# Two graph-attention layers: dense products of both layers in pieces of 512 columns that run across the relations

## The chip, the cores and the metric

The kernel runs on one core of a Trainium2 chip. The metric is the device time of one execution in microseconds, as a median over runs. A core has five engines with queues of their own: PE (TensorE, the matrix products; its weight loads are listed apart as PEld), DVE (VectorE), ACT (ScalarE), POOL (GpSimd) and SP (SyncE, which only issues transfers here). Each engine works through its queue in order and waits for others by semaphores.

## The reference

x has 3125 nodes of 768 features. There are 53125 edges (source, destination, relation 0 to 2, sorted by destination). Two layers of relational graph attention follow one another, then x is added and a layer norm taken. One layer, cut to what matters:

```python
xr = jnp.einsum('nd,rdf->rnf', x, W)          # three relations, 768 x 768 each
oi, oj = xr[etype, dst], xr[etype, src]
alpha = leaky_relu(oi @ q + oj @ k, 0.2)      # per edge and head
e = jnp.exp(alpha - segment_max(alpha, dst)[dst])
a = e / (segment_sum(e, dst)[dst] + 1e-16)
out = segment_sum(a[:, :, None] * oj.reshape(-1, heads, out_ch), dst) + b
```

Layer 1 has four heads of 192 columns, layer 2 one head of 768. Between them stands an elu. The dense product `xr` is the largest piece of arithmetic: 3125 x 768 times 768 x 2304 in each layer.

## The kernel before

**Blocks and stages.** The nodes are cut into 25 blocks of 128 (NB). Four stages follow one another: preparation (`weights_kq`, `nodes_kq`), `phase1` (dense product of layer 1, attention weights of layer 1), `phase2` (sums of layer 1 over the edges, elu, dense product of layer 2) and `phase3` (attention weights and sums of layer 2, layer norm). The order of all instructions is written out by hand: each stage is a loop over small steps, a table `ev` holds what is emitted at which step, and every engine executes its share in that order.

**A dense product.** A float32 product is made of three products in fp32r: a high part of x times a high and a low part of W (`wH`, `wL`), and a low part of x times the high part of W. The 768 rows of W make six tiles (DT), so one output piece takes 6 x 3 = 18 matmuls into one PSUM buffer `po`, of which there are two. `wH` and `wL` hold W as [128, 18 tiles, 770]. A piece has half the columns of one relation (384), so a block takes 3 relations x 2 halves x 18 = 108 matmuls. In layer 2 the first half of each relation is 386 wide: columns 384 and 385 hold W2·k and W2·q.

**Layer 1** (`phase1`, loop over n). One step emits one piece: `d_group` (L724) emits 18 matmuls, and `d_row` in the next step emits ACT's copy of the piece to a row buffer (L743) and, after the second half, SP's store of the row to `tab1` (L745). Rows have 772 columns: per head 192 and a one. Three row buffers rotate. Each sixth matmul is made to wait for one of the indirect gathers of attention keys that POOL issues meanwhile (L479), the same fraction along their list. Block b's x is transposed by `d_turn` (L701) and split into high and low by `d_split` (ACT L708, DVE L709). Between the pieces PE, DVE and ACT make the attention weights (`a_index` to `a_put`); `a_back` (L683) transposes what ACT's exp (L679) made behind two DVE scans. The last four blocks run relation by relation, so that each relation's part of `wH` and `wL` comes free and can take W2. `w_split` splits W2 and stores it to `w2_d` earlier; `second_weights` loads it in twelve transfers on ACT's queue (L532), four for each relation, and DVE puts `wkq2` into columns 384 and 385 (L534, L535). Block 0's layer-1 product is made in `nodes_kq` (L403) in pieces of 384.

**Layer 2** (`phase2`, loop over k, one gathered slot of 128 edges per step, 17 steps per block). POOL gathers rows of `tab1`; DVE makes selection matrices (`high`, L471); PE multiplies them with the gathered rows into `acc` (`sums`, L978), in two batches per block. When a block's second batch is done, a chain of small steps makes its h: DVE `e_y` (L986 to L991), ACT `e_x` (L997), DVE `e_h` (L1022, L1023) giving `ey`, PE `e_t` (six transposes, L1030), ACT `e_s` (L1037) and DVE `e_s2` (L1043), which give the high and the low half of `hT`. Then its dense product starts (`d_part`, L1055): 18 parts per block, six matmuls each, spread over 17 steps. `d_part` of the block before is emitted between the links of this chain, since a block's parts run from six steps behind its own chain's start to five steps behind the next one's. `d_row` copies a piece to one of three row buffers (L1063), DVE picks the query column (L1067), SP stores the row to `tab2` (L1069).

**Layer 2's sums** (`phase3`) gather rows of `tab2` and multiply them in the same way (L1260, L1272), 386 columns twice.

Of the kernel before, what the change touches and what calls it, by code (L numbers as in the profile page):

```python
# [60 lines left out]
def kernel(  # L61
# [85 lines left out]
    wkq2 = keep.tile([P, R * DT, 2], F32, name="wkq2")  # L147
# [149 lines left out]
    def weights_kq(buf, work, psum, bank, kqr, wk, kqs, wH, wL, nodes, more):  # L297
# [8 lines left out]
        def turn(m):  # L306
            raw = [buf["W", 2 * m + c] for c in range(2)]
            pts = transposes(psum, raw)
            for c in range(2):
                i = 2 * m + c  # L310
                S.copy(wH[:, i, :D], raw[c])
                (V if i % 3 == 2 else G).tensor_sub(wL[:, i, :D], raw[c], wH[:, i, :D].bitcast(F32))
                buf.free("W", i)
            return split_parts(work, pts, 2 * P)
# [33 lines left out]
    def nodes_kq(buf, pre, work, psum, bank, wk, kqs, wH, wL, qq, more, edges_ready):  # L348
# [43 lines left out]
        def first(i):  # L392
# [8 lines left out]
            for t in (2 * i, 2 * i + 1):  # L401
                for n, (a, w) in enumerate(((tH, wH), (tH, wL), (tL, wH))):
                    T.matmul(po[g][:, :HALF], a[:, t % 2, :], w[:, r * DT + t, c * HALF:(c + 1) * HALF],  # L403
                             start=(t == 0 and n == 0), stop=(t == DT - 1 and n == 2))
# [121 lines left out]
    def second_weights(r, wH, wL):  # L526

        i = slice(r * DT, (r + 1) * DT)
        w = w2_d[r * DT * P:(r + 1) * DT * P, :].rearrange("(i p) (s c f) -> p s i c f", p=P, s=2, c=2)
        for c in range(2):  # L530
            for s, o in ((0, wH), (1, wL)):
                nc.scalar.dma_start(o.bitcast(F32)[:, i, c * HW:c * HW + HALF], w[:, s, :, c])  # L532
                yield
        V.tensor_copy(wH[:, i, HALF:HW], wkq2[:, i])  # L534
        V.tensor_sub(wL[:, i, HALF:HW], wkq2[:, i], wH[:, i, HALF:HW].bitcast(F32))  # L535


    def phase1(pre, work, psum, wH, wL, qq):
# [175 lines left out]
        def d_group(n, b, r, c):  # L714

            g, k = divmod(n, 6)
            po = psum.tile([P, 512], F32, name="po", bufs=2)
            xT = xt[b]
            n = 0
            for t in range(DT):  # L720
                i = r * DT + t
                sl = slice(c * HALF, (c + 1) * HALF)
                for s, w in ((0, wH), (0, wL), (1, wH)):
                    m = T.matmul(po[:, :HALF], xT[:, s, t, :], w[:, i, sl], start=(n == 0), stop=(n == 3 * DT - 1))  # L724
                    if n % 6 == 0:
                        tc.add_manual_dep(m.ins, gathered[slot((18 * g + 3 * k + n // 6) * NE // (3 * len(groups)))].name,
                                          behind, reason="an even load")
                    n += 1
            st["po", b, r, c] = po

        n_rows = []
        row_of = {}

        def d_row(b, r, c):
            po = st.pop(("po", b, r, c))
            if c == 0:
                n_rows.append(b)
                row_of[b, r] = rows[len(n_rows) % 3] if (b, r) != (NB - 1, R - 1) else share[3]
                if (b, r) == (NB - 1, R - 1):
                    V.memset(share[3].rearrange("p (h f) -> p h f", h=H1)[:, :, F1:CW], 1.0)  # L740
            o = row_of[b, r]
            to = o.rearrange("p (h f) -> p h f", h=H1)[:, 2 * c:2 * c + 2, :F1]
            S.copy(to, po[:, :HALF].rearrange("p (h f) -> p h f", h=2))  # L743
            if c == 1:
                nc.sync.dma_start(  # L745
                    tab1[b * P * R:(b + 1) * P * R, :].rearrange("(p r) f -> p r f", r=R)[:, r, :], o)
                if b == 1:

                    nc.sync.dma_start(tab2[N * R:, :].rearrange("(p r) f -> p r f", r=R)[:, r, :], o)
# [12 lines left out]
        def w_split(i):  # L762
            w = w2.pop(i)
            hl = work.tile([P, 2, D], F32R, name="w2hl", bufs=1)
            S.copy(hl[:, 0, :], w)
            V.tensor_sub(hl[:, 1, :], w, hl[:, 0, :].bitcast(F32))
            for s in range(2):
                j = work.tile([P, D], BF, name="w2j", bufs=1)
                V.scalar_tensor_tensor(j, w, 1.0, kq2[:, s, :], op0=ALU.mult, op1=ALU.mult,
                                       accum_out=wkq2[:, i, s:s + 1])  # L770
# [35 lines left out]
        groups = [(b, r, c) for b in range(1, GB) for r in range(R) for c in range(2)]  # L806
        groups += [(b, r, c) for r in range(R - 1) for b in range(GB, NB) for c in range(2)]
        groups += [(b, R - 1, c) for c in range(2) for b in range(GB, NB)]
# [3 lines left out]
        turn = [base(b) * len(groups) // NE for b in range(NB - LATE)]  # L812
# [32 lines left out]
        last_w2 = second_weights(R - 1, wH, wL)  # L845
        for n in range(max(ev) + 1):
# [15 lines left out]
            if m in (9, 17):  # L862
                w2s = second_weights(m // 16, wH, wL)
            if 9 <= m < 25:
                next(w2s, None)
            if m in (21, 22):
                next(last_w2)
# [5 lines left out]
            if n < len(groups):  # L873
                d_group(n, *groups[n])
            if 0 < n <= len(groups):
                d_row(*groups[n - 1])
            if n == len(groups):
                next(last_w2)
                next(last_w2)
        return last_w2  # L880


    def phase2(work, psum, wH, wL, last_w2):
# [1124 lines left out]
```

## Time and profile before

| | |
|---|---|
| median of 3 runs | 1987.32 us (1985.41 to 1988.5) |
| profiled execution | 1984.63 us, span 1982.8 us |
| PE busy | 1680.7 us, 85% |
| DVE busy | 1201.9 us, 61% |
| ACT busy | 376.5 us, 19% |
| POOL busy | 1333.2 us, 67% |
| DMA | 506.48 MB, mean 255 GB/s |
| chain that ended last | PE 60%, issue 10%, POOL 8%, DMA 7%, DVE 5% |
| of it dense products | layer 2 (L1055) 25%, layer 1 (L724) 20% |

The page's fifth part lists groups of instructions: line, engine, operation, tiles and shapes, count, then busy time, mean duration of one, and the engine's idle time before them. A matmul's duration there (344 ns for 386 columns) contains its way through the array; in a stream the next one ends sooner, so the distance between neighbours tells what one costs.

Times in the timeline count from the start of the span. Layer 1's products run from about 123 to 655 us, layer 2's from 691 to 1397, and layer 2's sums from 1401 to the end.

### The profile page before, as it was taken

The page shows a single profiled execution, that of the slowest core. Times are in us where ns is not written, and L with a number is a line of the kernel's source. Part 1 is how long each engine was busy: PE and PEld are TensorE (multiplying, and loading weights), DVE is VectorE, ACT ScalarE, POOL GpSimd, SP SyncE. Part 2 cuts the span into 40 slices and gives each one's busy share as a digit, 9 for nine tenths or more (in the row PEclk, how much of TensorE's full clock was granted, in tenths as well). Part 3 has the DMA queues.
Part 4 walks back from the last instruction along what each step waited for, and adds up shares of the span by engine and source line. Part 5 has one row for each costly group of instructions (what it writes and reads, how often), then busy time and mean ns, then how long its engine had stood idle before and what let it go on. Part 6 is the DMA issues. An engine that isn't in the chain of part 4 may idle for free.

```text
span 1982.8 us, 41452 instructions
## 1 busy us (share of the span) xinstructions
PE 1680.7 (85%) x14727; PEld 1406.6 (71%) x14727; DVE 1201.9 (61%) x4296; ACT 376.5 (19%) x661; POOL 1333.2 (67%) x1326
## 2 busy tenths in 40 slices
PE   6989999999999599999999999999465556556664
PEld 6979999999999489898989999899222223223322
DVE  6544555555554667767776777774456665666564
ACT  5421222221221011111111111111011211121111
POOL 4247777777771467777777776652577777777773
PEclk8989999999999899999999999999677777777777
DMA  7556545554557988888888888886799999999994
GB/s 196 191 122 189 179 162 187 170 167 159 182 186 242 365 274 272 294 271 278 272 297 268 276 273 297 271 277 215 252 322 334 331 334 347 335 318 317 327 321 145
DMA packets 161018, 506.48 MB, mean 255 GB/s; under 512 B 47925, under 2 KB 61244, under 8 KB 160803
## 3 DMA queue, kind: packets, MB, share of 16 engines
q0 software_dynamic: 81904, 331.52, 50.6%
q1 hardware_dynamic: 67101, 156.21, 22.3%
q10 hardware_dynamic: 11798, 16.00, 2.5%
q8 instruction: 120, 1.97, 0.4%
q14 instruction: 95, 0.78, 0.1%
HBM read 412.74 MB, written 95.69 MB: 256 GB/s over the span
## 4 chain that ended last, share of the span: by engine, by line
PE 60%; issue 10%; POOL 8%; DMA 7%; DVE 5%; ACT 1%; POOLq 0%; DVEq 0%; ACTq 0%; SPq 0%
PE po L1055 25%; PE po L724 20%; PE acc L978 10%; POOL G L479 8%; DMA G<-ftab,ridx 6%; PE acc L1260 2%; PE pt L1030 1%; DVE selp L471 1%; PE px L701 1%; PE acc L1272 1%; DVE share L674 0%; DVE F L1219 0%; DMA share<-ftab,rfirst 0%; DVE share L675 0%; DVE sT L624 0%
## 5 line engine op out<-in xcount | busy, mean ns | idle before, releaser
L1055 PE MATMUL po<-wH,hT 128*128 128x386 f32 (+1 forms) x1800 | 485.0, 344 | 3.1 <-DVE hT L1043 2.2
L479 POOL DMA_INDIRECT kt<-kt,ridx x374 | 397.4, 1062 | 113.9 <-issue 106.6
L479 POOL DMA_INDIRECT G<-ftab,ridx x374 | 376.2, 1006 | 113.9 <-issue 99.3
L724 PE MATMUL po<-wH,xT 128*128 128x384 f32 x1584 | 435.7, 346 | 5.5 <-ACT share L743 2.4
L471 DVE TENSOR_SCALAR selp<-frow,fdl,pall 128x32 f32<-128x32 f32 (+1 forms) x1688 | 384.0, 321 | 0.7 <-PE acc L978 0.7
L1055 PEld LDWEIGHTS po<-wH,hT 128*128 128x128 f32 x1800 | 330.5, 189 | 18.8 <-issue 14.7
L479 POOL DMA_INDIRECT share<-ftab,ridx x239 | 239.2, 1001 | 100.7 <-PE acc L978 47.4
L1055 PE MATMUL po<-wL,hT 128*128 128x386 f32 (+1 forms) x900 | 305.6, 340 | 0.0
L724 PEld LDWEIGHTS po<-wH,xT 128*128 128x128 f32 x1584 | 292.9, 190 | 9.3 <-ACT share L743 4.2
L724 PE MATMUL po<-wL,xT 128*128 128x384 f32 x792 | 269.5, 340 | 0.0
L1260 PE MATMUL acc<-G,selp 128*32 128x386 f32 x2292 | 249.2, 584 | 6.6 <-DVE selp L471 6.6
L1260 PEld LDWEIGHTS acc<-G,selp 128*32 128x32 f32 x2292 | 126.8, 128 | 102.7 <-issue 53.7
L479 POOL DMA_INDIRECT g<-ftab,ridx x135 | 135.2, 1001 | 64.5 <-PE acc L978 34.0
L978 PE MATMUL acc<-share,selp 128*32 128x193 f32 x3088 | 165.7, 330 | 13.5 <-DVE selp L471 11.1
L1063 ACT COPY r<-po 128x386 f32<-128x386 f32 (+1 forms) x150 | 72.3, 482 | 550.5 <-PE po L1055 550.5
L1055 PEld LDWEIGHTS po<-wL,hT 128*128 128x128 f32 x900 | 170.6, 190 | 0.0
L724 PEld LDWEIGHTS po<-wL,xT 128*128 128x128 f32 x792 | 151.1, 191 | 0.0
L978 PEld LDWEIGHTS acc<-share,selp 128*32 128x32 f32 x3088 | 114.0, 111 | 48.0 <-issue 22.0
L1171 DVE TENSOR_SCALAR sT<-bc,cols 128x512 bf16<-128x512 f32 (+1 forms) x125 | 82.5, 660 | 89.4 <-PE bc L1165 89.4
L743 ACT COPY share<-po 128x384 f32<-128x384 f32 x144 | 68.0, 479 | 298.9 <-PE po L724 278.2
L1165 PE MATMUL bc<-d,one 1*128 1x512 bf16 (+1 forms) x125 | 50.1, 400 | 87.2 <-DVE sT L1171 86.1
L978 PE MATMUL acc<-g,selp 128*32 128x193 f32 x1688 | 102.8, 328 | 1.5 <-DMA g<-ftab,rfirst 1.5
(288 smaller groups left out, 1923.5 us busy)
## 6 DMA issues: line engine op xcount, KB each, us to landing
ftab<-share SPq DMA_DIRECT2D x75, 386.0 KB
ftab<-r SPq DMA_DIRECT2D x75, 386.0 KB
share<-in_L_gnn_W_dram SPq DMA_DIRECT2D x36, 384.0 KB
w_d<-w2hl SPq DMA_DIRECT2D x18, 768.0 KB
sT<-dr_d SPq DMA_DIRECT2D x25, 534.0 KB
share<-in_x_dram SPq DMA_DIRECT2D x27, 384.0 KB
xb_d<-share SPq DMA_DIRECT2D x25, 384.0 KB
xr<-in_x_dram SPq DMA_DIRECT2D x21, 384.0 KB
```

The costliest lines, as they stand in the source:

```text
L471: V.tensor_scalar(sel.rearrange("p (t f) -> p t f", f=32), of, dl[:, b, j:j + 1], p, op0=ALU.is_equal, op1=ALU.mult)
L479: return G.indirect_dma_start(out=to, out_offset=None, in_=tab, in_offset=_index(i[:, j:j + 1]), bounds_check=NP * R - 1, oob_is_err=False)
L701: T.transpose(pt[:, t // 3, (t % 3) * P:(t % 3 + 1) * P], xr[:, t * P:(t + 1) * P], ident)
L724: m = T.matmul(po[:, :HALF], xT[:, s, t, :], w[:, i, sl], start=(n == 0), stop=(n == 3 * DT - 1))
L743: S.copy(to, po[:, :HALF].rearrange("p (h f) -> p h f", h=2))
L978: T.matmul(acc[32 * t:32 * t + 32, h // 2, c], sel[:, h, 32 * WINDOW[i].index(t):][:, :32], g[:, h * CW:(h + 1) * CW], start=(i == u[0] an ...
L1030: T.transpose(pt[:, t // 3, (t % 3) * P:(t % 3 + 1) * P], s["ey"][:, t * P:(t + 1) * P], ident)
L1055: T.matmul(po[:, :wd], hT[:, k, t, :], w[:, r * DT + t, sl], start=(t == 0 and n == 0), stop=(t == DT - 1 and n == 2))
L1063: S.copy(o[:, c * HW:c * HW + wd], po[:, :wd])
L1165: T.matmul(bc[:, :n], one, s["d"][:, 4 * i * P:4 * i * P + n], start=True, stop=True)
L1171: V.tensor_scalar(s["sT"][:, 4 * i * P:4 * i * P + n], bc[:, :n], cols[:, b:b + 1], None, op0=ALU.is_equal)
L1260: T.matmul(acc[32 * t:32 * t + 32, c, :HW], st[b, j][:, 32 * WINDOW[j].index(t):][:, :32], gs[:, (base(b) + j) % NG, c * HW:(c + 1) * HW], ...
```

## The change

`wH` and `wL` become [128, 6 tiles, 2310]: in each tile six columns for W·k and W·q (KQ = 6, k in reversed order of relations), then the 768 columns of each relation one after another. The dense products go over these columns in pieces of 512 whatever the relation: 512, 512, 512, 512, 256 in layer 1 and 512, 512, 512, 512, 262 in layer 2 (there with the six columns in front). A block takes 5 x 18 = 90 matmuls. In layer 1 a step emits 15 of them, in layer 2 a part emits five. `d_row` cuts a piece at relations and, in layer 1, at heads; a piece's copy in layer 1 is emitted six matmuls behind its last one. The layer-1 dependences on gathers stand at each fifth matmul. Rows of `tab2` now begin with the key column, then 768 columns, then the one. W2 is loaded in six column parts of two transfers each, behind the pieces of the last four blocks, and `wkq2` is copied once. In those blocks five row buffers rotate, and `d_turn` and `d_split` of the last three come in successive steps.

```diff
-    def second_weights(r, wH, wL):
+    def second_weights(r, f, n, wH, wL):
+        w = w2_d[r * DT * P:(r + 1) * DT * P, :].rearrange("(t p) (s f) -> p s t f", p=P, s=2)
+        for s, o in ((0, wH), (1, wL)):
+            nc.scalar.dma_start(o.bitcast(F32)[:, :, KQ + r * D + f:][:, :, :n], w[:, s, :, f:f + n])
+            yield
...
-        def d_group(n, b, r, c):
...
+        PIECES = [(f, min(512, R * D - f)) for f in range(0, R * D, 512)]
+        def d_products(groups):
+            made = 0
+            for b, (f, n) in groups:
+                po = psum.tile([P, 512], F32, name="po", bufs=2)
+                xT = xt[b]
+                i = 0
+                for t in range(DT):
+                    for s, w in ((0, wH), (0, wL), (1, wH)):
+                        m = T.matmul(po[:, :n], xT[:, s, t, :], w[:, t, KQ + f:KQ + f + n], start=(i == 0),
+                                     stop=(i == 3 * DT - 1))
+                        if made % 5 == 0:
+                            k = made // 5 * NE // (3 * STEPS)
+                            tc.add_manual_dep(m.ins, gathered[slot(k)].name, behind, reason="an even load")
+                        i += 1
+                        made += 1
+                        yield
+                due.append((made + 6, b, f, n, po))
...
+        later = share[:3] + [share[6], share[3]]
+        def d_row(b, f, n, po):
+            got = 0
+            for r, at, m in segments(f, f + n, D):
+                if at == 0:
+                    if b < GB:
+                        row_of[b, r] = rows[r]
+                    else:
+                        row_of[b, r] = later[len(n_rows) % 5]
+                        n_rows.append(b)
+                o = row_of[b, r]
+                for h, at_, k in segments(at, at + m, F1):
+                    if at_ == 0 and k == F1 and h % 2 == 0 and at + m >= (h + 2) * F1:
+                        S.copy(o.rearrange("p (h f) -> p h f", h=H1)[:, h:h + 2, :F1],
+                               po[:, got:got + 2 * F1].rearrange("p (h f) -> p h f", h=2))
+                    elif not (at_ == 0 and k == F1 and h % 2 and at <= (h - 1) * F1):
+                        S.copy(o[:, h * CW + at_:h * CW + at_ + k], po[:, got:got + k])
+                    got += k
...
+        STEPS = 6 * (NB - 1)
+        groups = [(b, p) for b in range(1, GB) for p in PIECES]
+        groups += [(b, p) for p in PIECES for b in range(GB, NB)]
...
+        w2s = {m: second_weights(r, f, n, wH, wL) for m, r, f, n in (
+            (7, 0, 0, 512), (11, 0, 512, 256), (13, 1, 0, 256), (16, 1, 256, 512), (21, 2, 0, 512), (25, 2, 512, 256))}
...
-            if m in (1, 3, 5):
-                d_turn(GB + 1 + m // 2)
-                d_split(GB + 1 + m // 2)
+            if m in (1, 2, 3):
+                d_turn(GB + m)
+                d_split(GB + m)
...
+            for u in (m, m - 1):
+                if u in w2s and m < 25:
+                    next(w2s[u])
...
+            for _ in range(15 if n <= STEPS else 0):
+                if next(products, 0) is None:
+                    made += 1
+                while due and (due[0][0] <= made or n == STEPS):
+                    d_row(*due.pop(0)[1:])
+            if n == STEPS:
+                next(w2s[25])
+                next(w2s[25])
...
+        PIECES = [(f, min(512, WW - f)) for f in range(0, WW, 512)]
+        def d_products(b):
+            s = blk[b]
+            hT = s["hT"]
+            for p, (f, n) in enumerate(PIECES):
+                po = s["po", p] = psum.tile([P, 512], F32, name="po", bufs=2)
+                i = 0
+                for t in range(DT):
+                    for k, w in ((0, wH), (0, wL), (1, wH)):
+                        T.matmul(po[:, :n], hT[:, k, t, :], w[:, t, f:f + n], start=(i == 0), stop=(i == 3 * DT - 1))
+                        i += 1
+                        yield
+        def d_part(b):
...
+            for _ in range(5):
+                next(s["parts"], None)
+        def d_row(b, p):
...
+            if p == 0:
+                s["q"] = work.tile([P, R], F32, name="q2", bufs=2)
+                s["k"] = work.tile([P, R], F32, name="k2", bufs=2)
+                V.tensor_copy(s["q"], po[:, :R])
+                V.tensor_copy(s["k"], po[:, R:KQ])
+            for r, at, m in segments(max(f, KQ) - KQ, f + n - KQ, D):
+                o = rows[r]
+                if at == 0 and r > 0:
+                    V.tensor_copy(o[:, 0:1], s["k"][:, R - 1 - r:R - r])
+                a = 1 if at == 0 and r == 0 else 0
+                got = KQ + r * D + at - f
+                S.copy(o[:, 1 + at - a:1 + at + m], po[:, got - a:got + m])
+                if at + m == D:
+                    nc.sync.dma_start(nodes(b, tab2.rearrange("(n r) f -> n r f", r=R))[:, r, :], o)
...
             for m in range(6 * R):
-                rc = divmod(m // 3, 2)
                 k = e + m * SL // (6 * R) if i else first + 5 + m * (SL + 3) // (6 * R)
-                when(k, d_part, b, *rc, m % 3)
-                if m % 3 == 2:
-                    when(k + 1, d_row, b, *rc)
+                when(k, d_part, b)
+                for p in range(len(PIECES)):
+                    if (18 * p + 17) // 5 == m:
+                        when(k + 1, d_row, b, p)
...
-                    T.matmul(acc[32 * t:32 * t + 32, c, :HW], st[b, j][:, 32 * WINDOW[j].index(t):][:, :32],
-                             gs[:, (base(b) + j) % NG, c * HW:(c + 1) * HW], start=(j == u[0]), stop=(j == u[-1]))
+                    T.matmul(acc[32 * t:32 * t + 32, c, :HALF + c], st[b, j][:, 32 * WINDOW[j].index(t):][:, :32],
+                             gs[:, (base(b) + j) % NG, 1 + c * HALF:][:, :HALF + c], start=(j == u[0]), stop=(j == u[-1]))
```

More of the change, by code (lines that the diff above doesn't have):

```diff
@@ L731, in phase1 @@
         n_rows = []
         row_of = {}
[L734 to L749, printed above, removed]
+        due = []
```

125 lines of the change are left out of this document (44 added, 81 removed).

## The prediction

> **What bounds the kernel now.** I read the table of stretches first. Its columns are the stretch, its length, then busy time and (in brackets) instructions of PE, PEld, DVE, ACT and POOL, the granted clock, DMA share and GB/s.
>
> ```profile
> 150.00:600.00 450.00, 441.89 (x2850) 430.32 (x2848) 240.06 (x711) 92.26 (x181) 350.78 (x326) 1.00 0.53 175
> 695.00:1000.00 305.00, 305.00 (x3322) 274.18 (x3322) 217.29 (x920) 47.16 (x84) 223.22 (x224) 1.00 0.84 278
> 1450.00:1980.00 530.00, 322.44 (x2882) 158.05 (x2880) 311.56 (x997) 92.11 (x118) 388.08 (x386) 0.73 0.89 314
> ```
>
> PE fills the layer-1 products (first row) and the layer-2 products (second) at full clock. The third stage, layer 2's sums, has DMA at 0.89 and PE idle for 40% of it. So the change acts where PE is the bound. Next, the chain of waits over one block of layer 2 (start, length, what, count):
>
> ```profile
> 825.15 4.09 PE acc L978 x96
> 829.24 5.47 PE po L1055 x30
> 834.71 0.75 PE pt L1030 x6
> 835.46 4.25 PE po L1055 x24
> 839.71 4.08 PE acc L978 x96
> 843.78 9.69 PE po L1055 x54
> 853.47 4.09 PE acc L978 x94
> ```
>
> One period is 28.32 us, from one second batch's end (829.24) to the next (857.56): 108 products, two batches of sums, six transposes. Then the timeline behind 829.24, with what the next block's products need:
>
> ```profile
> 829.79 1.39 DVE L991 SCALAR_TENSOR_TENSOR y<-acc,rz,fbias 128x192 f32<-128x192 f32 x4
> 831.10 1.97 DVE L471 TENSOR_SCALAR selp<-frow,fdl,pall 128x64 f32<-128x64 f32 x8
> 832.84 0.63 DVE L1022 TENSOR_SCALAR ey<-ey 128x768 f32<-128x768 f32 x1
> 833.51 0.96 DVE L1023 SCALAR_TENSOR_TENSOR ey<-y,ey 128x768 f32<-128x768 f32 x1
> 834.58 0.64 PEld L1030 LDWEIGHTS pt<-fident,ey 128*128 128x128 f32 x6 [0.19 <-issue]
> 835.49 0.80 ACT L1037 CAST hT<-pt 128x768 fp32r<-128x768 f32 x1 [1.27 <-PE pt L1030]
> 836.32 0.96 DVE L1043 TENSOR_TENSOR hT<-pt,hT 128x768 fp32r<-128x768 f32 x1
> 837.60 0.38 PEld L1055 LDWEIGHTS po<-wH,hT 128*128 128x128 f32 x2
> ```
>
> This is the latency that the products hide. DVE works without a pause from the sums' end until `ey` is ready at 834.47; the transposes start 0.11 us later, after a gap of 0.19: PE already waits a little. ACT makes the high half of `hT` by 836.29, DVE the low half by 837.28. The first product that needs the low half is a block's third; its weights load at 837.60, 0.32 later. There is almost no slack here. Last, the time of one product by width, in the PE timeline (two products per row) and the chain, and the layer-1 waits:
>
> ```profile
> 68.32 0.40 PE L293 MATMUL bank<-tH,wk 128*128 128x256 f32 x2
> 69.51 0.41 PE L293 MATMUL bank<-tL,wk 128*128 128x256 f32 x2
> 1375.91 21.13 PE po L1055 x120
> PE pa L683 <- ACT e L679: 7.6, 12, 2.1
> 662.43 1.00 POOL L479 DMA_INDIRECT share<-ftab,rfirst  x1 [55.78 <-DMA wL<-w_d]
> ```
>
> 256 columns: ten products from 68.32 to 69.51, 119 ns each (119.5 over several such runs). 384: 21.13/120 = 176 ns. Widths of 384 and 386 show no difference.
>
> **The change, part by part.**
>
> *Price of a 512-column product.* No row has one in such a stream. From 256 to 384 the price rises 56.5 ns, so a straight line gives 232.5. The bare stream can be estimated from layer 2's sums, f32 products, which I take to pass each column twice: 28 of them (386 columns, four side by side) take 2.81 us at 1454.8 with a drain of 0.57, so 320 ns a group (nearly twice 176), 160 a pass, 0.416 ns a column. The surplus over that is 13 ns at 256 columns and 16 at 384. If it stays 16, 512 columns cost 229.3; if the price goes by columns from 384, 234.7. I take 232.5, because the surplus did grow between the two widths.
>
> *Layer 1* (24 blocks, blocks 1 to 24). Five pieces of 512, 512, 512, 512 and 256 replace six of 384: 4 x 232.5 + 119.5 = 1049.5 against 6 x 176 = 1056 ns for each of 18 passes. That is 6.5 x 18 x 24 = -2.8 us (-8.3 at 229.3, +1.0 at 234.7).
>
> The code runs in steps, now of 15 products. Four steps in six last about 3.49 us instead of 3.17, and one, all in the narrow piece, 1.8. PE's waits here are mostly for ACT's exp behind two DVE scans: by the last-but-one row `a_back` (L683) waits 7.6 us in 12 waits, and thrice a late eviction adds 0.95 (as at 362.63). In the timeline these fall in the long steps, where each gains 0.3 us of cover; what hangs on the short step has 3.8 us of slack or more there and loses 1.4. I count -5 (0 to -7).
>
> ACT copies rise from 6 to 12 per block, since a piece is cut by head and relation. At 0.48 us for 384 columns and 0.80 for 768, a copy is about 0.16 plus 0.83 ns a column: 3.8 instead of 2.9 us per block on an engine 19% busy. The tight place is the fourth piece: its two copies (0.75 us) must end within the narrow fifth (18 x 119.5 = 2.15 us), or the next block waits for PSUM. ACT is usually 0.1 us behind PE, so I charge nothing; the dear end is a rival below.
>
> In the last four blocks three `d_turn` calls come one step apart, and block 22's product starts three products behind its transposes: the split (0.80 on ACT, 0.96 on DVE) shows for about 1 us, the next for 0.2, so +2 with some DVE lateness (0 to +4).
>
> The dependences on gathers keep their pace: 432, each behind the same fraction of 354 gathers. POOL's last key gather ends at 606.7 (662.43 less the idle 55.78) and PE's last product at 655, a lead of 48 us that covers a few.
>
> *Between the layers.* The 12 loads of W2 keep their bytes and move on ACT's queue; the last two shrink from 1152 to 768 KB each. At the 373 GB/s of 640 to 670 us that is -2.1. Against it, the part before (2 x 1536 KB) is issued 5.4 us before the last product and needs 8.4, and the four last row stores on SP come 2.15 instead of 3.2 us apart. The gathers start 7.4 us after the last product now (662.43). I take 0, bounds -2 and +3. Five row buffers rotate in these blocks: a buffer is reused 18 products (4.2 us) after its row's last copy, and its store must land by then. The copies of `wkq2`, three pairs of about 0.15 us on DVE, become one pair: nothing.
>
> *Layer 2.* The pieces are 512 x 4 and 262 (119.5 + 2.5 = 122): 4 x 232.5 + 122 = 1052 against 1056 ns, by itself -1.8 us in all. But the narrow piece is the last of a block, and a block's last products are the cover of the latency shown above. Work it through from 829.24:
> - Before the transposes stand 25 products (17 wide, 8 narrow), 17 x 232.5 + 8 x 122 = 4.93 us, where 30 took 5.28. `ey` still comes at 834.47, so the transposes start at 834.58 as now; PE only waits longer.
> - Behind them stand 10 narrow products, 1.22 us instead of 2.11. PE reaches the new block at about 836.36, with the high half barely there; after two wide products (0.47) it stops for the low half, which lands at 837.28. The weights load at 837.40, the third product runs from about 837.51, where it now runs from 837.77: 0.26 ahead.
> - From there to the next second batch 53 wide products remain, 12.32 us, where 64 took 11.26: +1.06. The sums are unchanged.
>
> So each period grows by 1.06 - 0.26 = 0.80 us. 23 periods give +18.4; the stretch ahead of the first, 55 x 232.5 for 66 x 176 ns, +1.2; the last block, where no picks delay DVE and nothing follows, -0.7. Sum +18.9 (14.4 at 229.3; 22 at 234.7). DVE gets four small copies instead of three (0.15 us each); one sits between `ey` and the low half now, and one will. DVE waits 2.91 us for a second batch, which covers the extra. ACT evicts 7 times instead of 6, inside long pieces. POOL needs 17 x 1.3 us, and up to 4 key gathers of 1.37, in a period of 28.3: no bound.
>
> *Layer 2's sums* read 384 and 385 columns instead of 386 twice, four bytes off: DMA bounds that stage, 0.
>
> **Sum.** -2.8 - 5 + 2 + 0 + 18.9 = +13.1. The profiled execution took 1984.63 us (span 1982.8): 1997.7. The median shown, 1987.32, lies 2.69 above it, so the forecast for a median is 2000.4.
>
> A rule to weigh: for a warm stream of one-pass matmuls the Trainium skill ("TensorE: Matmul & The Clock Gate", Back-to-back issue gap) gives N/2.4 + 2.5 ns. The trace does not agree: that would be 162.5 at 384 columns, where it shows 176. By the rule 512 columns take 215.8.
>
> **Rivals.**
> 1. *The surplus shrinks to 2.5 ns at 512 columns*, as for the f32 transposes of 128 columns (six in 0.64 us, 109 ns each, against 2 x 128 x 0.416 = 106.5 of stream). A product takes 215.8: layer 1 -31.7, layer 2 -3.5 (53 x 215.8 = 11.44 us, nearly the 11.26 of now), sum -38.2: 1949.1. This is the case on the other side. Each ns of the wide product is worth 4 x 18 x 24 in layer 1 and some 1340 in layer 2, 3.07 us; so below 228.2 ns the change wins. Against it: the surplus grew from 256 to 384. Chance 0.04. By the Trainium skill's rule above (same page and section) it would come out so.
> 2. *The surplus is fixed, 229.3 ns*: -8.3 - 5 + 2 + 14.4 = +3.1: 1990.4, hardly to be told from no change. Chance 0.13.
> 3. *The latency stays covered*, if DVE's part gets shorter by 0.8 us. Then layer 2 gives -1.8: sum -7.6, 1979.7. Against it: DVE runs without a pause there and nothing of it changes. Chance 0.05.
> 4. *The narrow piece also stalls layer 1*: in the timeline 33 of 144 evictions start over 0.3 us behind their last product, many by 4. If five blocks have that at the fourth piece, each waits 4 + 0.75 - 2.15 = 2.6 us: +13, so 2013. Against it: the late ones mostly stand in the first three steps of a block. Chance 0.14.
>
> The forecast has 0.64, with a range of its own of 1991 to 2011 from the bounds of the width and the waits. The range that leaves about 2 in 10 out is 1986 to 2014. A difference of 0.2% (4 us) is about what can be told from no change. Faster: rivals 1 and 3, 0.08 with rounding; same: most of rival 2 and the forecast's low tail, 0.13; slower 0.79.
>
> **What would show it.** The chain in layer 2 should show a period near 29.1 us, waits of PE at the transposes near 0.5 us and at the low half near 0.5 us in every block, and wide products 232 to 233 ns apart. In layer 1 the wait of `a_back` should shrink. A wide product under 228 ns, or a period under 28.3, makes the forecast wrong; so do new waits of PE for ACT's row copies in layer 1.

## The result and the profile after

The changed kernel takes 1989.72 us (median of 22 runs, 1987.21 to 1992.61), the kernel before beside it 1985.28 (22 runs, 1982.39 to 1991.05): a ratio of 1.0019 with an interval of 1.0013 to 1.0026, so 2.6 to 5.2 us slower. Forecast were +13.1. The profiled execution after took 1988.29 us (span 1986.3) against 1984.63 (1982.8). Its stages, cut at the first and last products and the first gathers, against the steps of the forecast:

| stage | before, us | after, us | change | forecast |
|---|---|---|---|---|
| layer 1, first to last product | 532.28 | 521.27 | -11.0 | -5.8 |
| from there to layer 2's first product | 36.31 | 37.35 | +1.0 | 0 (-2 to +3) |
| layer 2, first to last product | 705.70 | 720.58 | +14.9 | +18.9 |
| of it 23 periods | 23 x 28.434 | 23 x 29.088 | +15.06 | +18.4 |
| layer 2's sums | 581.8 | 580.2 | -1.6 | 0 |

So layer 2 lost, layer 1 won, and the forecast had the loss too large (by 4.0 us) and the gain too small (by 5.2). The table of stretches after, with the columns of the one before (PE, PEld, DVE, ACT, POOL, clock, DMA share, GB/s):

```profile
150.00:600.00 450.00, 447.28 (x2520) 371.55 (x2519) 243.80 (x724) 101.22 (x313) 350.96 (x326) 1.00 0.56 184
695.00:1000.00 305.00, 301.59 (x3025) 233.78 (x3025) 213.37 (x912) 47.44 (x95) 218.36 (x220) 1.00 0.83 272
1450.00:1980.00 530.00, 325.08 (x2902) 159.66 (x2902) 315.75 (x1010) 93.64 (x120) 389.77 (x390) 0.73 0.89 316
```

In layer 1 PE's gaps shrink (447 of 450 us, 442 before), in layer 2 it has gaps now (301.6 of 305, none before). The third stage stands as it was. The chain of waits over one period of layer 2 after (start, length, what, count), from one second batch's end (822.68) to the next (851.73):

```profile
818.48 4.21 PE acc L1004 x96
...
823.12 1.39 DVE y L1017 x4
824.51 1.88 DVE selp L475 x8
826.39 0.41 DVE ey L1048
826.83 0.97 DVE ey L1049
827.80 0.04 issue
827.84 0.89 PE pt L1056 x6
828.75 0.81 ACT hT L1063
829.59 0.97 DVE hT L1069
830.56 0.04 issue
830.60 2.13 PE po L1082 x8
832.73 4.08 PE acc L1004 x96
836.81 10.71 PE po L1082 x45
847.52 4.21 PE acc L1004 x92
```

Before, this chain held PE alone. Now, for 8 of the 29 us, it runs through the links that make `ey` and `hT`: PE no longer has work until they are done. PE's weight loads in layer 2 name the same two links, each in nearly all of the 24 blocks that follow another (waited for, us in total, times, longest):

```profile
PEld po L1082 <- DVE hT L1069: 15.2, 24, 0.6
...
PEld pt L1056 <- DVE ey L1049: 8.0, 23, 0.4
```

In layer 1, PE's waits over 120 to 660 us, before:

```profile
PE po L724 <- ACT share L743: 2.8, 4, 0.8
```

and after:

```profile
PE pa L689 <- ACT e L685: 4.3, 6, 2.1
```

The wait for the exp fell from 7.6 (its line stands in the prediction) to 4.3 us, and the products' wait for ACT's row copies, which stood second before, is no longer listed. These lists leave out idle times of PE of 0.15 us and less.

### The profile page after: what moved, and what is told of

Its sections match the earlier page's. It is cut to its first block, busy times and chain, and to the rows that moved or that the text cites. A ratio compares the mean times of both kernels' runs of the same rounds, so it can differ in the third digit from the quotient of the medians.

```text
span 1986.3 us, 39880 instructions
## 1 busy us (share of the span) xinstructions
PE 1685.1 (85%) x13845; PEld 1246.3 (63%) x13845; DVE 1198.2 (60%) x4318; ACT 384.2 (19%) x830; POOL 1332.4 (67%) x1326
## 4 chain that ended last, share of the span: by engine, by line
PE 58%; DVE 12%; issue 10%; POOL 9%; DMA 8%; ACT 2%; POOLq 0%; SPq 0%; ACTq 0%; DVEq 0%
PE po L731 22%; PE po L1082 17%; PE acc L1004 10%; POOL G L483 8%; DMA G<-ftab,ridx 6%; DVE selp L475 3%; PE acc L1300 2%; DVE y L1017 2%; PE bank L295 1%; DVE hT L1069 1%; PE pt L273 1%; DVE ey L1049 1%; DMA e<-in_edge_type_dram 1%; PE po L407 1%; PE pt L1056 1%
## 5 line engine op out<-in xcount | busy, mean ns | idle before, releaser
L1082 PE MATMUL po<-wH,hT 128*128 128x512 f32 (+1 forms) x1500 | 440.7, 378 | 7.0 <-DVE hT L1069 6.2
L731 PE MATMUL po<-wH,xT 128*128 128x512 f32 (+1 forms) x1320 | 407.1, 382 | 2.3 <-ACT xT L714 1.1
L1082 PEld LDWEIGHTS po<-wH,hT 128*128 128x128 f32 x1500 | 271.8, 189 | 68.3 <-DVE hT L1069 17.4
L1082 PE MATMUL po<-wL,hT 128*128 128x512 f32 (+1 forms) x750 | 286.0, 381 | 0.0
L731 PEld LDWEIGHTS po<-wH,xT 128*128 128x128 f32 x1320 | 244.0, 191 | 49.0 <-ACT xT L714 2.0
L1300 PE MATMUL acc<-G,selp 128*32 128x384 f32 (+1 forms) x2292 | 249.2, 584 | 6.6 <-DVE selp L475 6.5
L731 PE MATMUL po<-wL,xT 128*128 128x512 f32 (+1 forms) x660 | 247.0, 374 | 0.0
L1082 PEld LDWEIGHTS po<-wL,hT 128*128 128x128 f32 x750 | 141.9, 189 | 38.7 <-issue 14.4
L1109 ACT COPY r<-po 128x262 f32<-128x262 f32 (+5 forms) x175 | 71.6, 436 | 403.0 <-PE po L1082 212.8
L475 DVE TENSOR_SCALAR selp<-row_p,fdl,p 128x32 f32<-128x32 f32 (+1 forms) x422 | 102.7, 317 | 0.9
```

The source lines that it names most:

```text
L475: V.tensor_scalar(sel.rearrange("p (t f) -> p t f", f=32), of, dl[:, b, j:j + 1], p, op0=ALU.is_equal, op1=ALU.mult)
L731: m = T.matmul(po[:, :n], xT[:, s, t, :], w[:, t, KQ + f:KQ + f + n], start=(i == 0), stop=(i == 3 * DT - 1))
L1082: T.matmul(po[:, :n], hT[:, k, t, :], w[:, t, f:f + n], start=(i == 0), stop=(i == 3 * DT - 1))
L1109: S.copy(o[:, 1 + at - a:1 + at + m], po[:, got - a:got + m])
L1300: T.matmul(acc[32 * t:32 * t + 32, c, :HALF + c], st[b, j][:, 32 * WINDOW[j].index(t):][:, :32], gs[:, (base(b) + j) % NG, 1 + c * HALF:][ ...
```

## The experiments: layer 2's narrow piece

Four kernels take the change apart. Their kernel before took 1986.01 us.

**Layer 1 alone** (layer 2 back to six pieces, in the changed kernel's layout and loops):

```diff
-        PIECES = [(f, min(512, WW - f)) for f in range(0, WW, 512)]
+        PIECES = [(f, n) for f, n in zip((0, 386, 770, 1156, 1540, 1926), (386, 384) * 3)]
...
-            for _ in range(5):
+            for _ in range(6):
...
```

> Layer 1 as changed; layer 2 keeps the new row layout and copies, but its 2310 columns are cut into six pieces of 386 and 384 again, six products to a part. Theory A (layer 2 loses because the narrow last piece bares the latency of ey and hT): the period of layer 2 is back at 28.4 us and the whole stands where layer 1 alone puts it, 11 us under the kernel before, about 1974 us. Rival B (the new layout, the copies or the row stores of layer 2 cost the time): the period stays near 29.1 and the whole near 1989.

Measured: 1972.4 us, ratio 0.9934 (0.9917 to 0.9951). Layer 1 takes 522.2 us, 10 less than before and nearly as in the changed kernel, where -5.8 were forecast. A period of layer 2 is 28.28 us and its whole 4 us shorter than before, so the pieces' new layout costs nothing there.

**Layer 2 alone** (layer 1 back to pieces of 384, 18 products to a step; the dependences stand at each sixth product again and W2's parts are 384 wide; the rest of the new loop kept):

```diff
-        PIECES = [(f, min(512, R * D - f)) for f in range(0, R * D, 512)]
+        PIECES = [(f, 384) for f in range(0, R * D, 384)]
...
-            for _ in range(15 if n <= STEPS else 0):
+            for _ in range(18 if n <= STEPS else 0):
...
```

> Layer 1 in pieces of 384, 18 products to a step, with the rest of the new loop (evictions six products late, five row buffers at the end, turns one step apart, W2 in six parts, these of 384 columns); layer 2 as changed. Theory A: layer 2 costs +15 to +16 us. Theory C (layer 1 gained through its long steps and 2.8 us of cheaper products): layer 1 takes about 532 us as before, the whole about 2001 us. Rival D (layer 1 gained through the new loop, whatever the width): layer 1 takes 522 to 525 us, the whole about 1992.

Measured: 2011.82 us, ratio 1.0115 (1.0093 to 1.0138), period 29.09 us. Layer 1 takes 543.4 us, 11 more than before; but from block 3's transposes to block 21's it takes 392.09 us, as before (392.93). The new loop thus brings nothing to layer 1 by itself. The 11 us lie at the ends: six products that take 0.63 to 1.16 us more than their price (5.8 in all) where the last blocks' `d_turn` now come one step apart, about 4 us at the stage's start, and the rest in small waits. So this kernel overstates the loss, and with it the two halves sum to more than the whole.

**Narrow piece first.** Layer 2's piece of 262 columns goes from the end of a block to its start; nothing else changes:

```diff
-        PIECES = [(f, min(512, WW - f)) for f in range(0, WW, 512)]
+        PIECES = [(0, WW - 4 * 512)] + [(f, 512) for f in range(WW - 4 * 512, WW, 512)]
```

> The changed kernel, with the narrow piece of layer 2 (262 columns) as a block's first instead of its last: the same 90 products. Theory A: behind the second batch stand 25 wide products (5.8 us) and ten more behind the transposes (2.3 us), so ey and both halves of hT are ready in time, the period is 28.2 us instead of 29.1, and the whole about 1969 us. Rival B: the order of the pieces does not matter, the period stays near 29.1 and the whole at 1989.

Measured: 1971.5 us, ratio 0.9923 (0.9907 to 0.994), period 28.26 us. As many products of the same widths, in another order, make 0.96% (19 us). The chain of waits of this kernel over a period is PE's alone again:

```profile
819.48 4.09 PE acc L1004 x96
823.57 6.02 PE po L1082 x25
829.58 0.65 PE pt L1056 x6
830.24 3.58 PE po L1082 x20
833.82 4.08 PE acc L1004 x96
837.90 9.78 PE po L1082 x45
```

The 25 products before the transposes are all wide here and last 6.02 us, while `ey` is ready 5.2 us behind the batch's end; the cover is back, with some to spare. With the kernel of layer 1 alone this shows the cause in layer 2: not the wide pieces, nor that they run across relations, but that the block's last pieces, which cover the next block's chain, had become short. This kernel also beats both kernels.

**Equal pieces** (five of 462 columns, `[(f, WW // 5) for f in range(0, WW, WW // 5)]`):

> The changed kernel with layer 2's 2310 columns cut into five equal pieces of 462 (no narrow piece at the end of a block); layer 1 as changed. By the line through 119.5 ns at 256 columns and 232.5 at 512 a product of 462 takes about 210 ns, so a block's 90 products take what they take now (18.9 us). Theory (the period grew because the block's last products, its cover, had become narrow): 25 products before the transposes give 5.25 us and 10 behind them 2.1, as in the kernel before, so the period falls from 29.09 to 28.2 to 28.4 us and the whole to 1970 to 1975 us. Rival (the period grew because pieces run across relations, with other copies and cuts): the period stays near 29.1 and the whole near 1989.

Measured: 2583.44 us for 2658.52 beside it, ratio 0.9733 (0.9682 to 0.9784), in executions in which the engines paused and every kernel took 28 to 34% longer (the last section). Once more:

> The changed kernel with five equal pieces of 462 columns in layer 2 once more, on another chip. Theory (the narrow last piece bared the latency): a period of 28.2 to 28.4 us and the whole 11 to 16 us less than the kernel before. Rival (pieces across relations cost by their copies and cuts): a period near 29.1 and the whole 2 to 5 us more than the kernel before.

2591.43 us for 2654.36, ratio 0.9699 (0.9654 to 0.9745), with pauses again. In another set with pauses the changed kernel itself stands at 0.9639, so these runs do not show what equal pieces are worth without the pauses. A product of 462 columns took about 210 ns there, where the line through 119.5 at 256 and 232.5 at 512 puts it.

## The experiments: where layer 1's gain came from

**Even steps.** A step of layer 1 ends after 18 x 384 columns and not after 15 products, so that all steps last as long as before; pieces and copies as changed, two of W2's loads a step later:

```diff
-            for _ in range(15 if n <= STEPS else 0):
-                if next(products, 0) is None:
-                    made += 1
+            more = n <= STEPS
+            while more and wide < 18 * HALF * (n + 1):
+                w = next(products, 0)
+                more = w > 0
+                made += more
+                wide += w
...
```

> The changed kernel, with layer 1's steps cut by columns (6912 to a step, what six passes of 384 times three were) instead of by 15 products, so that all steps last about 3.15 us. Theory C (the waits of layer 1 shrank because five of six steps are 0.3 us longer): the waits behind ACT's exp come back, layer 1 takes 526 to 530 us instead of 521, the whole 1994 to 1998 us. Rival D: layer 1 stays at 521 and the whole at 1989.

Measured: 1997.64 us, ratio 1.006 (1.0044 to 1.0077), layer 1 524.1 us. Three microseconds of layer 1's gain go; the larger part stays. (Of the 8 us that this kernel takes over the changed one, 2.8 lie in layer 1; in the profiles 3.1 more lie ahead of layer 1 and 2.3 in layer 2's sums, where the two kernels have the same instructions.) PE's waits in layer 1 of this kernel:

```profile
PE pa L689 <- ACT e L685: 6.9, 12, 2.1
```

The waits for the exp are back at 12, but those for the row copies are not. So two things won, and only one is the length of a step.

The timelines show the other. Before, at a late exp (start, length, engine, line, what):

```profile
361.17 0.31 ACT L679 ACTIVATE e<-e 72x128 f32<-72x128 f32 x1 [7.07 <-DVE e L678]
361.39 0.81 ACT L765 CAST w2hl<-share 128x768 fp32r<-128x768 f32 x1
361.53 0.28 PE L683 MATMUL pa<-fident,e 72*128 72x72 f32 x1 [0.53 <-ACT e L679]
362.07 1.00 POOL L479 DMA_INDIRECT kt<-kt,ridx  x1 [0.30 <-issue]
362.11 0.85 ACT L743 COPY share<-po 128x384 f32<-128x384 f32 x2
...
362.63 0.44 PE L724 MATMUL po<-wH,xT 128*128 128x384 f32 x1 [0.81 <-ACT share L743]
```

After, at the same exp:

```profile
355.79 0.31 ACT L685 ACTIVATE e<-e 72x128 f32<-72x128 f32 x1 [6.05 <-DVE share L681]
...
356.15 0.29 PE L689 MATMUL pa<-fident,e 72*128 72x72 f32 x1 [0.22 <-ACT e L685]
356.24 0.48 PE L731 MATMUL po<-wH,xT 128*128 128x512 f32 x1
```

Before, ACT stood idle for 7 us ahead of the exp, the last 4 of them with a finished piece to copy (its last product ends at 357.18); but the copy was behind the exp in its queue (here behind W2's split too), and the next product needed that piece's PSUM buffer. It starts 0.05 us after the first copy's end (362.58), 1.10 behind the transposes of the exp. In the kernel before, products follow 15 such transposes; at ten of them the first product starts 0.36 to 1.10 us behind the transposes, each time 0.05 us after a copy's end. What these ten start later than 0.10 us behind the transposes sums to 5.2 us. After, the product starts 0.06 to 0.09 us behind the transposes every time, and the sum is gone: by the order of the code, only one of a block's five pieces still ends where a step ends, with the next step's exp queued ahead of its copy. The kernel of layer 2 alone, which emits its copies six products late as the changed one does but whose pieces end with the steps, keeps ten such delays, 5.2 us; so the later emission by itself is not what won.

**Copies first, in the kernel before.** If that reading is right, moving each copy ahead of its step's attention work takes this wait away:

```diff
+            if 0 < n <= len(groups):
+                d_row(*groups[n - 1])
...
             if n < len(groups):
                 d_group(n, *groups[n])
-            if 0 < n <= len(groups):
-                d_row(*groups[n - 1])
```

> The kernel before with the copy ahead of the step's attention work, for its layer-1 time without pauses of PE. Theory (the copy stands behind the late exp and PE needs its buffer): layer 1 about 527 us for 532.3, the whole 4 to 5 us less than the kernel before. Rival: 531 to 532, and the whole within 1 us. With pauses the ratio to the kernel before should again lie between 0.995 and 0.998.

Measured: 1984.48 us against 1988.11 beside it, ratio 0.9983 (0.9974 to 0.9991): 1.8 to 5.2 us less. The product now starts 0.09 to 0.10 us behind the transposes at every late exp. But layer 1 takes 530.8 us in the profile, where about 527 were expected (and the profiled execution, 1984.9 us, is no shorter than the one before). PE waits longer for the exp itself, and once for a gather at the stage's start:

```profile
PE pa L683 <- ACT e L679: 9.9, 13, 2.3
PE po L724 <- DMA kt<-kt,rfirst: 3.2, 1, 3.2
```

So the wait was what I took it for, but in this profile most of what its removal saved was lost again elsewhere. In the 18 blocks of the table below the products' time falls by 5.0 us, while 2.9 come back at the exps and 0.8 in the rest. Of the 2.9, 1.6 stand at one exp:

```profile
230.23 0.84 ACT L765 CAST w2hl<-share 128x768 fp32r<-128x768 f32 x1 [2.06 <-DMA share<-in_L_gnn_W_dram]
231.10 0.96 DVE L766 TENSOR_TENSOR w2hl<-share,w2hl 128x768 fp32r<-128x768 f32 x1 [2.38 <-ACT w2hl L765]
...
237.16 0.28 PE L683 MATMUL pa<-fident,e 72*128 72x72 f32 x1 [1.88 <-ACT e L679]
```

A load of W2 landed late there, ACT's split waited for it, and DVE, behind the split, came late to the scans. Whether the edit or this one execution made the load and the gather late is not shown.

The same kernel ran in four sets with pauses as well. The first:

> The kernel before, where each step of layer 1 emits ACT's copy of the piece before it ahead of the step's attention work, and not behind it; nothing else moves. Theory (a third of layer 1's waits before came from ACT's copy being caught behind the late exp, so that PE, back from its wait for the exp, found no free PSUM buffer): the waits of PE for the exp stay near 7.6 us, the waits of the products behind them fall from 13 to about 8, layer 1 takes 527 to 529 us for 532.3, and the whole 3 to 5 us less than the kernel before, 1981 to 1983. Rival (only the length of a step counts, as cover of the exp): layer 1 stays at 532 and the whole at 1985 to 1987.

2644.47 us for 2658.52, ratio 0.9976 (0.9939 to 1.0013). The second:

> The kernel of the copy ahead of the step's attention work once more, on another chip, since on the first one every kernel, the kernel before too, took a third more time, with pauses of PE that no wait explains. Theory (a third of layer 1's waits before came from ACT's copy being caught behind the late exp, so that PE found no free PSUM buffer): the waits for the exp stay near 7.6 us, those of the products behind them fall from 13 to about 8, layer 1 takes 527 to 529 us for 532.3, the whole 3 to 5 us less than the kernel before. Rival (only the length of a step counts, as cover of the exp): layer 1 stays at 532 and the whole within 1 us of the kernel before.

2648.77 for 2654.36, ratio 0.998 (0.995 to 1.001). The third:

> The kernel of the copy ahead of the step's attention work, on a chip that does not pause. In the trace of the kernel before, the first product behind a late a_back starts 0.05 us after ACT's copy of an earlier piece has ended and 0.36 to 1.10 after a_back's start; those delays sum to 4.9 us. Theory (the copy stands behind the late exp in ACT's order, and PE needs its buffer): with the copy ahead of the exp that product starts 0.1 us after a_back, the late a_back waits stay (10 of them), layer 1 takes about 527 us for 532.3, the whole 4 to 5 us less than the kernel before. Rival (the delay only moves to another wait behind it): layer 1 stays at 531 to 532 and the whole within 1 us.

2663.9 for 2667.1, ratio 0.9983 (0.9955 to 1.001); where no pause falls in between, the product starts about 0.10 us behind the transposes here too, as the theory has it. The fourth:

> The kernel before with the copy ahead of the step's attention work. On a chip without pauses: layer 1 takes about 527 us for 532.3 and the whole 4 to 5 us less than the kernel before (theory: the copy stands behind the late exp and PE needs its buffer), or 531 to 532 and the whole within 1 us (rival). On a chip where PE pauses the run adds to three intervals of 0.998 and decides nothing by itself.

2653.43 for 2656.87, ratio 0.9949 (0.9905 to 0.9992). All four lean the way of the run without pauses; only the last excludes 1 by itself.

The account of PE's time from block 3's transposes to block 21's (18 blocks, each operation counted from the end of the one before it to its own) puts the two together:

| kernel | stretch, us | products | exp's transposes | all else |
|---|---|---|---|---|
| before | 392.93 | 353.45 | 6.96 | 32.52 |
| changed | 381.88 | 346.01 | 3.39 | 32.48 |
| layer 2 alone | 392.09 | 352.86 | 6.80 | 32.43 |
| even steps | 384.94 | 346.17 | 6.30 | 32.48 |
| copies first | 391.63 | 348.42 | 9.87 | 33.34 |

Of the change's -11.05 us, -3.57 are waits for the exp, and even steps give 2.9 of them back: that is cover by longer steps. -7.44 are products: their price is 339.8 us (1296 at 232.4 ns and 324 at 119.3) for 341.8 (1944 at 175.8), so -2.0, and -5.4 are waits ahead of them, 4.3 of these the delays behind the exp. Copies first gives 5.0 less in the same column.

**A third PSUM buffer** for layer 1's pieces; the bank for it comes from putting the index transposes into free columns of the tile `pq`:

```diff
+        pq = psum.tile([P, 2, 512], F32, name="pq", bufs=1)
...
-            pT = s["pi"] = psum.tile([P, 512], F32, name="pT", bufs=1)
+            pT = s["pi"] = pq[:, 0, 400:]
...
-                po = psum.tile([P, 512], F32, name="po", bufs=2)
+                po = psum.tile([P, 512], F32, name="po", bufs=3)
...
```

In the kernel before:

> The kernel before with three PSUM buffers for layer 1's pieces in place of two (the bank comes from putting the index transposes into unused columns of another PSUM tile of the stage); order and products unchanged. Theory (late copies hold PE through the PSUM buffer): the waits of the products behind the exp fall from 13 to about 8 us, layer 1 takes 527 to 529 us for 532.3, the whole 1981 to 1983. Rival (the buffer was free in time, and the gaps behind the exp are something else): layer 1 stays at 532, the whole at 1985 to 1987. If sharing the tile adds a wait of the index transposes, layer 1 becomes longer than 532.3 and the run tells nothing on this.

Measured, with pauses: 2652.99 us for 2658.52, ratio 1.0019 (0.9972 to 1.0066). Again:

> The kernel before with three PSUM buffers for layer 1's pieces once more, on another chip. Theory (late copies hold PE through the PSUM buffer): layer 1 takes 527 to 529 us for 532.3, the whole 3 to 5 us less than the kernel before. Rival (the buffer was free in time): layer 1 stays at 532 and the whole within 1 us of the kernel before.

2653.14 for 2654.36, ratio 0.9993 (0.9965 to 1.0021), with pauses too. It tells nothing on this. In the kernel with the narrow piece first:

> The changed kernel with the 262-column piece first in layer 2 and three PSUM buffers in layer 1. Theory: wide pieces already ask for a new buffer only every 4.2 us, so a third one has little left to give: layer 1 519 to 522 us for 522.8 with two, the whole 1968 to 1971 for 1971.5. If the remaining waits of the products in the changed kernel (7.8 us) are waits for PSUM too, layer 1 falls to 516 and the whole to 1965.

With pauses: 2542.99 us for 2658.52, ratio 0.9605 (0.9556 to 0.9655), and in the next set:

> The changed kernel with the 262-column piece first in layer 2 and three PSUM buffers in layer 1 once more, on another chip. Theory: a third buffer has little left to give where wide pieces ask for one only every 4.2 us: layer 1 519 to 522 us for 522.8 with two, the whole 14 to 18 us less than the kernel before. If the remaining waits of the products in the changed kernel (7.8 us) are waits for PSUM too, layer 1 falls to 516 and the whole by 20 us.

2543.32 for 2654.36, ratio 0.9584 (0.9554 to 0.9614). Without pauses:

> The changed kernel with the 262-column piece first in layer 2 and three PSUM buffers in layer 1. Without pauses: layer 1 519 to 522 us for 522.8 with two buffers, the whole 14 to 18 us less than the kernel before; 516 and 20 us if the changed kernel's remaining waits are waits for PSUM. With pauses the ratio should again be near 0.96.

Measured: 1979.12 us, ratio 0.9959 (0.9946 to 0.9972), so slower than with two buffers (0.9923). Layer 1 takes 529.1 us, and its waits say why:

```profile
PE pq L643 <- DVE n_all L596: 4.6, 5, 2.9
PE pq L643 <- DVE lim L587: 3.1, 3, 1.0
```

The shared tile makes the attention work's products wait for DVE's reading of the index transposes. The dense products take 346.04 us in the stretch above, as with two buffers (346.01 in the changed kernel): in wide pieces a third buffer has nothing left to give.

## Why the prediction was right and wrong

- **Price of a wide product**: forecast 232.5 ns; the ends of neighbours lie 232.5 apart in layer 1 and 232.8 in layer 2. Rivals 1 (215.8) and 2 (229.3) fall with it. No run shows that f32 products pass each column twice, as the estimate of the bare stream took them to, and its 160 ns over 386 columns are 0.4145 ns a column and not 0.416 (0.3 ns less for rival 2); the sum used neither. For the Trainium skill's N/2.4 + 2.5 ns ("TensorE: Matmul & The Clock Gate", Back-to-back issue gap), which the section gives for an isolated matmul, the trace does not agree at 512 columns either: 232.5 where it gives 215.8.
- **Layer 1's products**, -2.8: -2.0 in 18 blocks is -2.7 in 24. Right.
- **Layer 1's waits, -5 (0 to -7): the step that failed.** Over the whole stage PE's time at the exp's transposes, each counted from the end of the operation before it, fell from 9.7 to 5.8 us, and the delays of the products behind them fell from 5.2 us to none: about -9, beyond the bounds. I had read the first in the list of waits and seen the three longest of the ten delays, and let the length of a step cover both. That every late exp holds back the copy queued behind it on ACT, and the copy the next product, I had not followed; even steps, which have no longer cover, keep that part of the gain.
- **`d_turn` in the last blocks**, +2: three waits of about 0.5, +1.5. Right.
- **Layer 2**, +18.9: the mechanism was right, waits of PE at the transposes and at the low half in every block (its weight loads waited 0.35 and 0.63 us there, for about 0.5 and 0.5 forecast), shown by the experiments that put the narrow piece elsewhere or take it out. The size was not: a period grew by 0.65 and not 0.80 us. The third product ends 8.89 us behind the batch's end before and 8.53 after, a lead of 0.36 where I had 0.26. I let the waiting PE begin its transposes 0.11 us after `ey` and the third product 0.23 after the low half; it begins 0.05 after each (827.84 behind 827.79, 830.60 behind 830.55). By its starts the third product's lead is even 0.53, but after the wait it takes 0.50 us to its end, where the one of 386 columns took 0.33. That the period of 29.1 us named as a sign came (29.09) is partly luck, for the block it was worked out from (28.32) is shorter than the mean (28.43). With the first stretch (+0.65 for +1.2) and the last block (-0.8 for -0.7) it is +14.9.
- **Between the layers**, 0: +1.0, within its bounds. **Layer 2's sums**, 0: -1.6; the kernels of layer 1 alone, layer 2 alone and narrow piece first, with that stage as changed, show 581.7, 581.7 and 580.8 beside 581.8 before, so an effect is not shown.
- **Rival 3** (the latency stays covered) is wrong for the changed kernel. **Rival 4** (the narrow piece stalls layer 1) is wrong: no wait of products for a row copy is left.
- **Sum**: 13.1 less 5.2 in layer 1, less 4.0 in layer 2, plus 1.0, less 1.6 gives 3.3; the spans of the two profiled executions differ by 3.4. The sum was too high on both sides of the balance: too small a gain, with half of its mechanism missing, and too large a loss, of the right kind.

## What to carry to other kernels

When products of one block cover the latency of the next, cost a new tiling by the time of the pieces that stand in that place, not by its mean: the order of the same five pieces decided 19 us. When an instruction is late, look at what is queued behind it on its engine and who needs that; here the copy behind the exp cost PE more than half as much as the exp itself. A wait taken out alone may be lost again in part at other waits of the same path, so value it by an experiment and not by the list of waits.

## What the runs showed of the hardware

In four sets of runs, on two chips (the second set ran on the chip of the first, though its expectations say another), every kernel took more time from the first dense product on: those that ran both ways 28 to 34% more, the kernel before 2654 to 2667 us. The preparation took its 122 to 125 us as ever; PE paused within streams of products, mostly where nothing that the profile shows was waited for. The shares of the chain of the kernel with copies first, in such an execution, and waits of its engines without a releaser in the profile:

```profile
PE 28%; issue 21%; DVE 11%; another core or an unknown queue 10%; POOL 8%; DMA 1%; ACT 1%; POOLq 0%; DVEq 0%; ACTq 0%
...
PE po L724 <- issue: 52.4, 69, 4.9
...
DVE q L1067 <- issue: 183.4, 30, 8.5
...
ACT share L743 <- issue: 126.3, 24, 13.6
```

Between neighbouring dense products it had 173 pauses of over 0.23 us beyond a product's price, 175 us in all (the kernel before without this: 4, 5 us). DVE and ACT paused too: from 125 us on, DVE sat idle for over 0.5 us without such a releaser 134 times and ACT 141 times, where the same kernel without pauses has 3 and 9. The granted clock was lower as well, 0.84 over 125 to 700 us and 0.92 over 925 to 1700, where the kernel before without pauses has 0.99 and 1.00 in its dense products. Whether that is a cause of the pauses or follows from them is not shown. There the change has the other sign:

> The changed kernel itself, beside the others. On a chip without pauses: 3 to 5 us more than the kernel before. On a chip where PE pauses between products: if the pauses go by the number of PE instructions (882 products of 14727 fewer), 2 to 4% less than the kernel before; if they go by the time, again 0.2% more.

> The changed kernel with the 262-column piece first in layer 2. On a chip without pauses 14 to 16 us less than the kernel before. On a chip where PE pauses: as many products as the changed kernel, so by their number the same 2 to 4% less, and by the bared latency of layer 2 some 15 us under the changed kernel.

The changed kernel stands at 0.9639 (0.957 to 0.9708) of the kernel before, and with the narrow piece first at 0.9563 (0.9491 to 0.9635); with three buffers besides, 0.9605 and 0.9584. Kernels with 13845 PE products stood at 0.956 to 0.973, those with 14727 at 0.995 to 1.002. In the changed kernel's execution 96 such pauses took 95 us (30 and 16 us without this). So under these pauses the kernels with fewer, wider products gain; whether it is their number that counts, two numbers of products cannot tell, since widths and copies change along with them. Nor is it shown whether the bared latency of layer 2 still costs: the narrow piece first took 11 us less in the same set, with intervals that overlap. What causes the pauses was not settled.
